# A gated cross-attention block on one core: the local stage's residual kept by tokens, the experts' outputs in halves, and free banks for the GLU

## The chip, the core and the metric

The kernel runs on one core of a Trainium2 chip. The core's engines are TensorE (PE, matrix products and transposes into the accumulator memory PSUM), VectorE (DVE), ScalarE (ACT), GpSimd (POOL) and SyncE (SP, which issues DMAs here). They run side by side, each through its own instructions in order, and wait for each other through semaphores. The metric is the device time of one execution in microseconds; lower is better.

## The reference

The input `x` is 16 batches (B) of 256 tokens (S) of 128 features (D). Everything is fp32. Four residual stages follow each other, each on the layer norm of `x` and scaled by tanh of a scalar gate:

```python
x = x + tanh(g_xattn[0]) * cross_attention_0(layernorm(x), ctx)   # 16 heads of 8, 64 keys
x = x + tanh(g_ffn[0])   * local_ffn(layernorm(x))
x = x + tanh(g_xattn[1]) * cross_attention_1(layernorm(x), ctx)   # with biases
x = x + tanh(g_ffn[1])   * experts(layernorm(x))

def local_ffn(x):                      # two layers of
    h = shift_token(x)                 # features 64..127 come from the token before
    q, k, v = split(h @ wqkv)          # 8 heads of 64
    q, k = rotary(l2norm(q) * qs, l2norm(k) * ks)
    x = x + window_attention(q, k, v) @ wo      # windows of 64 tokens
    h = layernorm(shift_token(x)) * lg + lb
    a, g = split(h @ w1 + b1)          # 341 hidden features each
    x = x + (a * gelu(g)) @ w2 + b2

def experts(x):                        # 4 experts of width 128, 4 of width 256
    w, sel = top_2(sigmoid(x @ router.T));  w = w / sum(w)
    return sum over the two chosen experts e of w_e * (relu(x @ w1_e)**2 @ w2_e)
```

All eight experts are computed for every token and weighted by `combine`, which is zero for those not chosen.

## The kernel before

The input stays in SBUF as `x_sb`, a tile of 128 tokens by 32 half batches by 128 features. One batch is two such half batches.

The order of the work is written into step tables (`CROSS_STEPS`, `LOCAL_STEPS`, `GLU_STEPS`, `EXPERT_STEPS` and others). A line names a step, the lag at which it runs behind its batch, its engine, a weight, the steps it needs, and the rooms (buffers or PSUM banks) that it takes, with the steps that give them back. `timetable` keeps one in-order queue of steps per stream (table) and engine, sorted by lag, and merges the streams greedily: whenever an engine is free it takes the first queue whose head has its needs and rooms, the earlier stream first. `play` issues the instructions in that order, so that each engine's order is fixed when the kernel is built. Three plays follow each other: the first cross attention, together with the preparation of weights and the first two norms of the local stage; the local stage; the second cross attention with the experts.

In the local play the streams are attention 0, GLU 0, attention 1, GLU 1, the other norms (`first`) and some clearing. A stream can be held until another has begun a step: `behind`. The GLUs are held until the attention of their layer has begun its last `scale1`; attention 1 is held until GLU 0 has begun the `shift` of the last batch.

The local stage's residual `yT` is kept transposed: features on partitions, 256 tokens of a batch along the free dimension. This is what each stage does with it, per batch:

- `first` norms `x_sb`, turns the result by two PE transposes (line 902) and copies it into `yT` on ACT (line 1176).
- Attention `shift` copies `yT` by two DMAs of SP (lines 1261 and 1262) into one of three `hbuf`, the second of them one token later. `qk` and `value` multiply it with `wqkv` (lines 1267 and 1297). At the end `project` (line 1445) multiplies the attention's result with `wo`, four matmuls of 256 columns, and `add` (line 1451) adds it to `yT`.
- GLU `shift` copies `yT` into one of two `gbuf` by two copies on POOL (lines 1245 and 1246). `hturn` transposes that back to tokens (line 902), `stat` (lines 1484, 1485) and `apply` (line 1495) make the norm from PSUM, `rstd` is on POOL (lines 1489, 1490), `nturn` transposes it again, `affine` is on ACT (line 1505), `up0` to `up2` (line 1521) are 12 matmuls of 256 columns, `gelu` and `gate` follow (lines 1531, 1539), `down` (line 1545) is three matmuls of 256 columns, and `out` (line 1551) adds it and the bias to `yT` on DVE.
- The last GLU also has `yturn`, which transposes `yT` to tokens, and `back` (line 1561), which adds it to `x_sb`.

Each fp32 matmul appears as two instructions in the trace. PSUM has banks named QK, SC, TR (two banks' width each), VB and OB. In the GLU's steady batches accumulator A (up0, up1) is always in QK, B (up2 and down) always in SC, and T, N and Y in other fixed ones.

In the experts `hid` makes 12 hidden blocks (line 1632), `out` (line 1654) multiplies them with the second weights, 24 instructions per half batch, into one tile of all eight experts. `sum` (line 1662) adds them to `x_sb` in eight DVE instructions, each an expert's output times its column of `comb`, and issues the output's DMA (line 1666).

Of the kernel before, what the change touches and what calls it, by code (L numbers as in the profile page):

```python
# [11 lines left out]
F32 = mybir.dt.float32  # L12
# [4 lines left out]
ALU = mybir.AluOpType  # L17
# [23 lines left out]
exp0 7 ACT 1.08 score_t pT:mix  # L41
mturn 2 PE 0.25 parts M:mturn_out
mturn_out 6 ACT 0.38 mturn mT:score_t
exp1 7 ACT 1.08 score_t,exp0
turn_out 4 ACT 0.38 turn xnT:query
rstd 2 POOL 1.03 stat
vals 5 POOL 0.32 - V:mix
refine 8 DVE 0.84 inverse
share 8 DVE 0.43 refine oT:project
log 7 ACT 0.38 mix  # L50
stat 2 DVE 0.92 - sm:apply
offset 3 DVE 0.16 rstd
top0 5 DVE 1.2 score
apply 2 POOL 1.02 offset xn:turn
score 1 PE 1.25 query_out,keys BIG:top0 BIG:top1
turn 0 PE 0.4 apply M:turn_out
keys 3 POOL 0.6 - Kd:score+score_t
mix 3 PE 1.8 exp0,exp1,vals O:share
inverse 7 ACT 0.38 log
top1 5 DVE 1.2 score,top0  # L60
parts 5 DVE 0.9 top0,top1 mp:mturn
add 8 DVE 0.48 project
query 0 PE 0.6 turn_out M:query_out
query_out 4 ACT 0.39 query QT:score+score_t
score_t 2 PE 1.2 mturn_out,query_out,keys BIG:exp0 BIG:exp1
project 4 PE 0.5 share M:add
"""

SECOND_STEPS = """
inverse 6 ACT 0.38 log  # L70
score 6 PE 1.25 query_out,keys BIG:top0 BIG:top1
apply 1 POOL 1.02 offset xn:turn
stat 3 DVE 0.92 - sm:apply
turn 5 PE 0.4 apply M:turn_out
top0 6 DVE 1.2 score
exp0 5 ACT 1.08 score_t pT:mix
mturn_out 4 ACT 0.38 mturn mT:score_t
exp1 5 ACT 1.08 score_t,exp0
mix 8 PE 1.8 exp0,exp1,vals O:share
rstd 0 POOL 1.03 stat  # L80
top1 6 DVE 1.2 score,top0
parts 6 DVE 0.9 top0,top1 mp:mturn
keys 0 POOL 0.6 - Kd:score+score_t
query 5 PE 0.6 turn_out M:query_out
offset 4 DVE 0.16 rstd
add 9 DVE 0.48 project
turn_out 2 ACT 0.38 turn xnT:query
score_t 7 PE 1.2 mturn_out,query_out,keys BIG:exp0 BIG:exp1
refine 8 DVE 0.84 inverse
share 8 DVE 0.43 refine oT:project  # L90
log 5 ACT 0.38 mix
vals 2 POOL 0.32 - V:mix
project 9 PE 0.5 share M:add
query_out 2 ACT 0.39 query QT:score+score_t
mturn 6 PE 0.25 parts M:mturn_out
# [3 lines left out]
hid2 4 PE 1.88 turn_out,hid1 BIG:relu2  # L99
stat 4 DVE 0.92 -  # L100
hid0 3 PE 1.88 turn_out BIG:relu0
prob 8 ACT 0.22 router
rstd 0 POOL 0.95 stat
apply 0 POOL 0.9 offset exn:turn
relu1 7 ACT 1.06 hid1,relu0
out0 5 PE 2.9 square0,square1,square2 BIG:sum0
turn_out 6 ACT 0.38 turn exnT:hid2+router
square0 7 ACT 1.04 relu0
sum1 8 DVE 1.95 out1,route
router 4 PE 0.45 turn_out O:prob  # L110
relu2 7 ACT 1.06 hid2,relu1
sum0 7 DVE 1.95 out0,route
out1 5 PE 2.9 square0,square1,square2 BIG:sum1
square2 7 ACT 1.04 relu2
square1 7 ACT 1.04 relu1
offset 4 DVE 0.16 rstd
route 6 DVE 2.7 prob cb:sum0+sum1
hid1 3 PE 1.88 turn_out,hid0 BIG:relu1
relu0 6 ACT 1.06 hid0 h:out0+out1
turn 2 PE 0.44 apply M:turn_out  # L120
# [4 lines left out]
xload0 6 LX 4.6 -  # L125
pturn 6 PE 0.35 pens BIG:pturn_out
cdup0 3 DVE 0.69 cturn0
pool 3 LP 5.0 -
cturn1 3 PE 0.9 cload1,cturn0 BIG:cturn_out1+cdup1
mload1 5 LM 7.0 mload0  # L130
vals2 9 PE 1.0 vals1,cdup1 BIG:vals_out2
vals1 6 PE 1.0 vals0 BIG:vals_out1
pturn_out 6 DVE 0.2 pturn
part 3 DVE 0.55 pload,dve
wload0 1 LW 5.4 -
fill1 9 DVE 0.65 mload1,fill0
keys_out1 8 ACT 0.61 keys1
wturn1 4 PE 0.4 wload1 BIG:wturn_out1
keys0 4 PE 1.8 wturn_out0,cturn_out0 BIG:keys_out0
fill0 7 DVE 0.28 part,mload0  # L140
heads 0 DVE 0.62 dve
wturn2 9 PE 0.25 wload2 BIG:wturn_out2
cturn_out1 1 ACT 0.61 cturn1
cturn_out0 0 ACT 0.61 cturn0
vals_out0 7 DVE 0.7 vals0
dve 1 LD 1.4 -
keys1 6 PE 0.95 cturn_out1 BIG:keys_out1
mload0 1 LM 7.0 -
wload1 1 LW 2.0 wload0
vals_out3 9 DVE 0.7 vals3  # L150
gates 7 ACT 0.3 act,pload
vals_out1 7 DVE 0.7 vals1
wturn_out0 0 ACT 0.38 wturn0
xload1 6 LX 2.0 xload0
wturn0 2 PE 0.8 wload0 BIG:wturn_out0
wturn_out1 2 ACT 0.25 wturn1
wturn_out2 9 ACT 0.25 wturn2
vals_out2 8 DVE 0.7 vals2
sels 5 DVE 0.3 heads
pload 2 LQ 6.2 -  # L160
cturn0 2 PE 1.0 cload0,wturn0 BIG:cturn_out0+cdup0
cload0 4 LC 5.4 -
keys_out0 3 ACT 0.61 keys0
unit 2 ACT 2.5 narrow,act
vals0 5 PE 1.3 wturn_out1,cdup0 BIG:vals_out0
narrow 0 DVE 0.38 dve
late 0 DVE 1.7 pool
nload 2 LN 10.0 -
cdup1 5 DVE 0.69 cturn1
cload1 4 LC 1.8 cload0  # L170
vals3 9 PE 1.0 vals2 BIG:vals_out3
wload2 1 LW 6.5 wload1
act 2 LA 3.0 -
pens 3 DVE 0.7 nload
# [3 lines left out]
keys1 2 PE 0.95 wturn_out BIG:keys_out1  # L178
vals_out3 3 DVE 0.7 vals3
rw 7 PE 0.15 - BIG:rw_out  # L180
vals2 9 PE 0.98 wturn_out BIG:vals_out2
vals_out1 5 DVE 0.7 vals1
cols 2 PE 0.15 - BIG:cols_out
keys_out1 2 DVE 0.75 keys1,cols_out
vals0 3 PE 0.98 wturn_out BIG:vals_out0
keys_out0 8 DVE 0.75 keys0,cols_out
vals_out0 3 DVE 0.7 vals0
rw_out 3 DVE 0.2 rw
bo_out 6 DVE 0.25 bo
bias 4 DVE 0.25 cols_out  # L190
vals1 7 PE 0.98 wturn_out BIG:vals_out1
bo 7 PE 0.4 bias,wturn_out BIG:bo_out
wturn 1 PE 0.6 - BIG:wturn_out
keys0 9 PE 0.95 wturn_out BIG:keys_out0
vals_out2 5 DVE 0.7 vals2
wturn_out 2 ACT 0.62 wturn
vals3 2 PE 0.98 wturn_out BIG:vals_out3
cols_out 0 DVE 0.35 cols
# [3 lines left out]
fill 3 DVE 1.2 -  # L202
local1 9 POOL 0.65 -
seen 0 DVE 1.0 -
tab2 9 DVE 0.5 -
tab3 3 DVE 0.5 -
tab1 3 DVE 0.5 -
local3 4 POOL 0.8 -
local0 1 POOL 0.98 -
tab0 8 DVE 0.5 -  # L210
local2 5 POOL 0.65 -
# [6 lines left out]
apply 1 POOL 0.9 offset hn:turn  # L218
turn 2 PE 0.3 apply VB:out
out 2 ACT 0.38 turn  # L220
# [9 lines left out]
add 5 DVE 0.42 project  # L230
norm0 2 POOL 0.87 root0
pturn_out1 5 ACT 1.02 pturn1 pT:mix1
mix_out0 5 ACT 0.62 mix0 oT:project
turn0 2 PE 0.995 scale0 TR:turn_out0
score1 3 PE 1.24 turn_out1,turn_out0 SC:exp1+top1
total0 3 DVE 1.4 exp0
pturn1 4 PE 1 share1 TR:pturn_out1
mix0 4 PE 1.07 pturn_out0,dma0 OB:mix_out0
share1 4 POOL 1.9 total1
scale0 2 POOL 1.05 rotate0,norm0  # L240
qk1 1 PE 1.75 shift QK:square1+sin1+cos1
rotate1 2 POOL 2.56 sin1,cos1
clip1 2 POOL 0.27 sums1
exp1 4 ACT 2.6 top1 pr:pturn1
dma0 8 DMA0 2.5 value_out0
value0 2 PE 0.911 shift VB:value_out0
pturn0 3 PE 1 share0 TR:pturn_out0
root0 2 ACT 0.45 clip0
sin0 1 DVE 1.21 qk0 u:rotate0
norm1 2 POOL 0.87 root1  # L250
shift 3 DMA2 2.6 - hb:qk0+qk1+value0+value1
cos0 1 DVE 1.21 qk0 qn:turn0
pturn_out0 4 ACT 1.02 pturn0 pT:mix0
mix1 4 PE 1.07 pturn_out1,dma1,dma0 OB:mix_out1
mix_out1 5 ACT 0.62 mix1,mix_out0
square1 2 ACT 1.04 qk1 sq:sums1
share0 3 POOL 1.9 total0
scale1 2 POOL 1.05 rotate1,norm1
top1 3 DVE 1.4 score1,norm1
clip0 1 POOL 0.27 sums0  # L260
turn_out1 3 ACT 1.02 turn1
score0 2 PE 1.24 turn_out0 SC:exp0+top0
rotate0 1 POOL 2.56 sin0,cos0
sums0 1 DVE 1.22 square0
turn1 2 PE 0.995 scale1 TR:turn_out1
sin1 1 DVE 1.21 qk1 u:rotate1
exp0 3 ACT 2.6 top0 pr:pturn0
value_out0 2 DVE 0.7 value0 v:mix0+mix1
project 4 PE 1.69 mix_out0,mix_out1 OB:add
total1 3 DVE 1.4 exp1  # L270
top0 2 DVE 1.4 score0,norm0
square0 1 ACT 1.04 qk0 sq:sums0
turn_out0 2 ACT 1.02 turn0 qT:score0+score1
root1 2 ACT 0.45 clip1
value1 2 PE 0.911 shift VB:value_out1
cos1 1 DVE 1.21 qk1 qn:turn1
qk0 0 PE 1.75 shift QK:square0+sin0+cos0
sums1 1 DVE 1.22 square1
value_out1 2 DVE 0.7 value1
dma1 9 DMA1 2.5 value_out1  # L280
"""
GLU_STEPS = """
up0 2 PE 0.96 affine A:gate0+gate1
gate0 4 DVE 0.48 gelu0
up1 2 PE 0.96 affine,up0
down 3 PE 1.45 gate0,gate1,gate2
gate1 4 DVE 0.48 gelu1,gate0
out 5 DVE 0.48 down
shift 6 POOL 1.25 - hg:hturn
rstd 7 POOL 0.95 stat  # L290
stat 2 DVE 0.92 hturn
gelu1 3 ACT 0.47 up1,gelu0
affine 2 ACT 0.5 nturn hnT:up0+up1+up2
gelu2 3 ACT 0.47 up2,gelu0
gelu0 2 ACT 0.47 up0 hh:down
nturn 1 PE 0.44 apply N:affine
gate2 4 DVE 0.48 gelu2,gate0
hturn 0 PE 0.44 shift T:apply
apply 2 DVE 0.82 rstd hn:nturn
up2 2 PE 0.95 affine B:out  # L300
"""
LAST_GLU_STEPS = """
gate1 2 DVE 0.48 gelu1,gate0
stat 0 DVE 0.92 hturn
rstd 3 POOL 0.95 stat
up1 2 PE 0.96 affine,up0
nturn 1 PE 0.44 apply N:affine
hturn 0 PE 0.44 shift T:apply
gelu2 5 ACT 0.47 up2,gelu0
gelu0 4 ACT 0.47 up0 hh:down  # L310
gate2 2 DVE 0.48 gelu2,gate0
up2 2 PE 0.95 affine B:out
apply 0 DVE 0.82 rstd hn:nturn
back 3 DVE 0.48 yturn
yturn 3 PE 0.44 out Y:back
shift 2 POOL 1.25 - hg:hturn
out 2 DVE 0.48 down
up0 1 PE 0.96 affine A:gate0+gate1
gate0 1 DVE 0.48 gelu0
# [1459 lines left out]
```

## Time and profile before

| what | value |
|---|---|
| times of three runs | 1162.91, 1167.99, 1166.86 us (median 1166.86) |
| profiled execution, its own time | 1164.6 us |
| its span in the profile | 1162.8 us |
| granted TensorE clock, mean | 0.989 |
| busy: PE / weight loads / DVE / ACT / POOL | 1080.4 / 786.3 / 940.2 / 734.9 / 630.9 us |
| DMA | 30.02 MB, mean 26 GB/s |

Stages by the trace: first cross attention until about 140 us, attention 0 until 430, GLU 0 until 517, attention 1 from 490 to 776, GLU 1 until 858, second cross attention until 989, experts from 957 to the end.

The profile was taken from one execution. Engine names are those above, PEld is TensorE's weight load, SPq the queue in which SP issues DMAs. "L1521" is line 1521 of the kernel before. In a timeline line the columns are start, duration, engine, line, operation, output from inputs, shapes, number of instructions, and in brackets the idle time of the engine before it with what ended it. In a line of windows each engine's busy time stands with its number of instructions, then the granted clock (1.00 is full), the DMA engines' busy share, and GB/s.

### The profile page before, as it was taken

What the parts mean: (1) busy time and instruction counts of PE and PEld (TensorE: products, weight loads), DVE (VectorE), ACT (ScalarE), POOL (GpSimd) and SP (SyncE); (2) the same over time, 40 slices, a digit from 0 to 9 for tenths busy, and PEclk for the clock granted to TensorE, in tenths of its full rate; (3) what the DMA queues carried; (4) which work ended last, traced back from release to release, by engine and by line L of the source; (5) the groups of instructions that cost most, each with busy time, mean ns of one, the idle gap of its engine ahead of it and who ended that gap; (6) DMA issues with size and microseconds to landing.
All of it is one profiled execution on the core that took longest, in us unless ns stands there. A gap on an engine that the chain in (4) does not pass through costs nothing.

```text
span 1162.8 us, 28289 instructions
## 1 busy us (share of the span) xinstructions
PE 1080.4 (93%) x11264; PEld 786.3 (68%) x11264; DVE 940.2 (81%) x2088; ACT 734.9 (63%) x1418; POOL 630.9 (54%) x1079
## 2 busy tenths in 40 slices
PE   7999878999999999888999999999979999999997
PEld 5555535766767777655667767677645557999996
DVE  7887679999999856679999999856757884777777
ACT  4555447888888863357888888853335557555462
POOL 5443179999988833258888888733345460111110
PEclk9999989999999999999999999999989999999999
DMA  6400011111111100001111111100000000000000
GB/s 182 143 2 2 10 24 33 33 29 38 37 31 36 29 10 10 1 14 33 37 30 37 38 34 33 29 7 1 1 1 2 2 1 2 12 13 12 13 12 17
DMA packets 29828, 30.02 MB, mean 26 GB/s; under 512 B 4668, under 2 KB 22656, under 8 KB 29696
## 3 DMA queue, kind: packets, MB, share of 16 engines
q1 hardware_dynamic: 28352, 27.56, 9.4%
q8 instruction: 89, 1.46, 0.5%
q10 hardware_dynamic: 1344, 0.66, 0.2%
q14 instruction: 43, 0.35, 0.1%
HBM read 9.33 MB, written 2.10 MB: 10 GB/s over the span
## 4 chain that ended last, share of the span: by engine, by line
PE 70%; DVE 18%; ACT 6%; issue 4%; POOL 1%; DMA 1%; SPq 0%; DVEq 0%; ACTq 0%; POOLq 0%
PE QK L1267 8%; PE e_y L1654 8%; PE e_h_ps L1632 7%; PE po L1115 5%; PE Ag L1521 4%; PE OB L1427 4%; PE TR L1415 3%; PE SC L1374 3%; ACT pr L1397 3%; DVE mx L1383 3%; PE VB L1297 3%; PE OB L1445 3%; PE TR L1346 3%; DVE qn L1278 3%; PE sT L1092 2%
## 5 line engine op out<-in xcount | busy, mean ns | idle before, releaser
L1397 ACT ACTIVATE pr<-SC,mx,rn 128x128 f32<-128x128 f32 x512 | 185.6, 468 | 36.1 <-DVE mx L1388 36.0
L1267 PE MATMUL QK<-wqkv,hbuf 128*128 128x512 f32 x256 | 129.5, 629 | 19.3 <-DVE qn L1278 14.2
L1410 POOL TENSOR_TENSOR pr<-pr,rs 128x1024 f32<-128x1024 f32 x64 | 121.4, 1896 | 14.7 <-DVE rs L1405 11.4
L1662 DVE SCALAR_TENSOR_TENSOR x_sb<-e_y,e_comb,x_sb 128x128 f32<-128x128 f32 x256 | 89.1, 349 | 21.6 <-PE e_y L1654 13.7
L1644 ACT ACTIVATE e_h<-e_h_ps 128x1024 f32<-128x1024 f32 x48 | 49.2, 1025 | 77.2 <-PE e_y L1654 61.8
L1267 PEld LDWEIGHTS QK<-wqkv,hbuf 128*128 128x128 f32 x256 | 44.6, 193 | 77.8 <-issue 40.2
L1654 PE MATMUL e_y<-mw,e_h 128*128 128x128 f32 x768 | 91.8, 277 | 0.0
L1632 PE MATMUL e_h_ps<-e_xnT,mw 128*128 128x256 f32 x384 | 89.8, 383 | 0.2
L1654 PEld LDWEIGHTS e_y<-mw,e_h 128*128 128x128 f32 x768 | 89.2, 192 | 0.7
L1040 DVE TENSOR_REDUCE nm<-sc 128x16 f32<-128x1024 f32 x64 | 75.0, 1214 | 14.2 <-PE sc L1031 14.0
L1275 ACT ACTIVATE sq<-QK 128x1024 f32<-128x1024 f32 x64 | 65.9, 1030 | 31.8 <-ACT pr L1397 9.0
L1312 POOL TENSOR_TENSOR qn<-qn,u 128x512 f32<-128x512 f32 x64 | 81.3, 1271 | 8.6 <-DVE qn L1278 6.0
L1278 DVE TENSOR_TENSOR u<-QK,tab 128x1024 f32<-128x1024 f32 x64 | 76.9, 1201 | 9.3 <-ACT sq L1275 5.4
L1102 ACT ACTIVATE xpT<-sT,penT 128x1024 f32<-128x1024 f32 x64 | 71.3, 1117 | 20.3 <-PE sT L1092 20.3
L1404 DVE TENSOR_REDUCE rs<-pr 128x8 f32<-128x1024 f32 x64 | 77.6, 1212 | 7.9 <-ACT pr L1397 5.3
L1383 DVE TENSOR_REDUCE mx<-SC 128x8 f32<-128x1024 f32 x64 | 77.5, 1212 | 6.3 <-PE SC L1374 6.3
L1313 POOL TENSOR_TENSOR qn<-qn,u 128x512 f32<-128x512 f32 x64 | 81.6, 1275 | 0.0
L1418 ACT COPY pT<-TR 128x1024 f32<-128x1024 f32 x64 | 64.4, 1007 | 24.0 <-PE TR L1415 24.0
L1278 DVE TENSOR_TENSOR qn<-QK,tab 128x1024 f32<-128x1024 f32 x64 | 77.6, 1213 | 1.1 <-ACT sq L1275 1.1
L1292 DVE TENSOR_REDUCE ss<-sq 128x16 f32<-128x1024 f32 x64 | 77.1, 1205 | 1.1 <-ACT sq L1275 1.1
L1632 PEld LDWEIGHTS e_h_ps<-e_xnT,mw 128*128 128x128 f32 x384 | 70.4, 190 | 10.9 <-DVE x_sb L1662 2.7
L1531 ACT ACTIVATE hhg<-Ag,cols 128x256 f32<-128x256 f32 x64 | 28.7, 472 | 72.7 <-PE Ag L1521 36.4
(217 smaller groups left out, 2644.8 us busy)
## 6 DMA issues: line engine op xcount, KB each, us to landing
vbuf<-vbuf SPq DMA_DIRECT2D x96, 128.0 KB
hbuf<-yT SPq DMA_DIRECT2D x32, 64.0 KB
out_dram<-x_sb SPq DMA_DIRECT2D x32, 64.0 KB
hbuf<-yT SPq DMA_DIRECT2D x32, 63.8 KB
wqkv<-in_L_ffn_wqkv_dram SPq DMA_DIRECT2D x2, 768.0 KB
mw<-in_L_ffn_w_dram SPq DMA_DIRECT2D x2, 768.0 KB
w<-in_L_ffn_w_dram SPq DMA_DIRECT2D x2, 341.0 KB
x_sb<-in_x_dram SPq DMA_DIRECT2D x1, 640.0 KB
```

The lines of the kernel that those rows point to most:

```text
L1267: nc.tensor.matmul(ps[:, 512 * j : 512 * j + 512], lhsT=hbuf[b % 3][:, W + t * P : W + (t + 1) * P], rhs=wqkv[:, l, 512 * j : 512 * j + 51 ...
L1278: nc.vector.tensor_tensor(work(tag, b, t, [P, 2, LH, LD], 2, wp), live["QK", b, t].rearrange("p (q h d) -> p q h d", q=2, h=LH), tab[:, l, ...
L1292: nc.vector.tensor_reduce(ss, live["sq", b, t].rearrange("p (g d) -> p g d", d=LD), AX.X, ALU.add)
L1312: nc.gpsimd.tensor_add(qg[:, :, 0:32], qg[:, :, 0:32], ug[:, :, 32:64])
L1313: nc.gpsimd.tensor_add(qg[:, :, 32:64], qg[:, :, 32:64], ug[:, :, 0:32])
L1383: nc.vector.tensor_reduce(mx, live["SC", b, t].rearrange("p (g c) -> p g c", c=P), AX.X, ALU.max, negate=True,)
L1397: nc.scalar.activation(pr[:, g, :], live["SC", b, t][:, g * P : (g + 1) * P], AF.Exp, bias=live["mx", b, t][:, g : g + 1], scale=live["rn" ...
L1404: nc.vector.tensor_reduce(rs, live["pr", b, t], AX.X, ALU.add)
L1410: nc.gpsimd.tensor_tensor(pr, pr, rs, ALU.mult)
L1632: nc.tensor.matmul(ps[:, c * S : (c + 1) * S], lhsT=mw1[:, (4 * j + c) * P : (4 * j + c + 1) * P], rhs=live["xnT", b], start=True, stop=True,)
L1654: nc.tensor.matmul(y[:, e * D : (e + 1) * D], lhsT=live["h", b][:, c, t * P : (t + 1) * P], rhs=mw2[:, c, :], start=(c == cs[0]), stop=(c ...
L1662: nc.vector.scalar_tensor_tensor(xt, live[f"y{t}", b][:, e * D : (e + 1) * D], live["comb", b][:, t, e : e + 1], xt, ALU.mult, ALU.add,)
```

## The change

It has five parts.

1. **The residual by tokens.** `yT` becomes `y_sb`, tokens on partitions as in `x_sb`. The first norms write `y_sb` directly, without transposes and ACT copy. In the attention the two DMAs are replaced by `hturn`, two PE transposes into bank VB, and `hout`, two ACT copies of 64 partitions into `hbuf`. `project` becomes eight matmuls of 128 columns with the weights as the moving side. In the GLU the copies on POOL and `hturn` are replaced by three DMAs of SP into `gbuf`, which now has tokens on partitions; `stat` and `apply` read `gbuf` in SBUF. `down` becomes six matmuls of 128 columns, the bias b2 is added to `y_sb` by a new step `bias` on POOL from a copy of b2 on all partitions (one more DMA at the start), `out` is a plain add, and `yturn` is gone: `back` reads `y_sb`.
2. **The GLU's accumulators** A and B take any of QK, SC and TR that is free (fewer at the two ends), N any of VB and OB.
3. **The release.** Attention 1 is held only until GLU 0 has begun its fifth `shift`.
4. **The experts' outputs in halves.** `out` becomes four steps, the narrow and the wide experts of each half batch. For each, `weigh` multiplies a half (128x512) with `comb`, broadcast, in one DVE instruction from PSUM into SBUF, and `gather` adds its four parts and `x_sb` in three POOL instructions; the output's DMA follows the second half. Four buffers for `weigh` (room `w`).
5. **All step tables are re-ordered**: new lags and rows, so the merge differs in places in every stage.

```diff
-    behind = (2 * l - 1, "shift", B - 1) if l else None
+    behind = (2 * l - 1, "shift", 4) if l else None
...
-    dict(A="QK", B="SC", T="VB", N="OB", Y="OB"),
+    (("QK", "SC"), ("TR", "VB")), (("QK", "SC", "TR"), ("VB", "OB")), (("TR", "SC"), ("OB", "VB")),
...
         # attention
-        def shift(b, t):
-            h = hbuf[b % 3]
-            nc.sync.dma_start(h[0:64, W : W + S], yT[0:64, b, :])
-            nc.sync.dma_start(h[64:128, W + 1 : W + S], yT[64:128, b, 0 : S - 1])
+        def hturn(b, t):
+            turn(acc("VB", b, t, 512), y_sb[:, b])
+        def hout(b, t):
+            h, ps = hbuf[b % 3], live["VB", b, t]
+            nc.scalar.copy(h[0:64, :], ps[0:64, 0:S])
+            nc.scalar.copy(h[64:128, 1:S], ps[64:128, 0 : S - 1])
...
         # GLU
         def shift(b, _):
-            shifted(yT, b, gbuf[b % 2])
-        def hturn(b, _):
-            turn(acc("T", b), gbuf[b % 2].rearrange("p (t q) -> p t q", t=2))
+            g, y = gbuf[b % 2], y_sb[:, b]
+            nc.sync.dma_start(g[:, :, 0:64], y[:, :, 0:64])
+            nc.sync.dma_start(g[1:P, :, 64:D], y[0 : P - 1, :, 64:D])
+            nc.sync.dma_start(g[0:1, 1, 64:D], y[P - 1 : P, 0, 64:D])
...
+        def bias(b, _):
+            y = y_sb[:, b]
+            nc.gpsimd.tensor_tensor(y, y, b2[:, l].unsqueeze(1).to_broadcast([P, 2, D]), ALU.add)
...
         def out_(b, _):
-            nc.vector.scalar_tensor_tensor(
-                yT[:, b, :], live["B", b][:, 512 : 512 + S], cols[:, 16 + l : 17 + l],
-                yT[:, b, :], ALU.add, ALU.add,
-            )
+            nc.vector.tensor_add(y, live["B", b][:, 512 : 512 + S], y)
...
         # experts
-        def sum_(b, t):
-            xt = x_sb[:, 2 * b + t, :]
-            for e in range(E):
-                nc.vector.scalar_tensor_tensor(
-                    xt, live[f"y{t}", b][:, e * D : (e + 1) * D], live["comb", b][:, t, e : e + 1],
-                    xt, ALU.mult, ALU.add,
-                )
-            nc.sync.dma_start(out_v[:, 2 * b + t, :], xt)
+        def weigh(b, j):
+            t, half = j // 2, j % 2
+            nc.vector.tensor_tensor(
+                work(f"w{j}", b, [P, 4, D], 4, wp, tag="e_w"),
+                live[f"y{t}", b][:, 512 * half : 512 * half + 512]
+                .rearrange("p (e d) -> p e d", e=4),
+                live["comb", b][:, t, 4 * half : 4 * half + 4].unsqueeze(2)
+                .to_broadcast([P, 4, D]), ALU.mult,
+            )
+        def gather(b, j):
+            w, xt = live[f"w{j}", b], x_sb[:, 2 * b + j // 2, :]
+            nc.gpsimd.tensor_add(w[:, 0:2, :], w[:, 0:2, :], w[:, 2:4, :])
+            nc.gpsimd.tensor_add(w[:, 0, :], w[:, 0, :], w[:, 1, :])
+            nc.gpsimd.tensor_add(xt, xt, w[:, 0, :])
+            if j % 2:
+                nc.sync.dma_start(out_v[:, 2 * b + j // 2, :], xt)
...
         # a step table, as an example: the GLU's lines for the steps around gbuf
-shift 6 POOL 1.25 - hg:hturn
-hturn 0 PE 0.44 shift T:apply
-stat 2 DVE 0.92 hturn
-apply 2 DVE 0.82 rstd hn:nturn
+shift 0 DMA2 2.8 - hg:apply
+stat 0 DVE 0.92 shift
+apply 1 DVE 0.6 rstd hn:nturn
```

In the changed kernel the room of a `gbuf` (`hg`, two of them) is given back by `apply`, since `stat` and `apply` read it directly; before it was given back by `hturn`.

## The prediction

> **What bounds the kernel now.** I read the page's busy times first, then the chain that ended last, then busy time by windows, one per stage.
>
> ```profile
> PE 1080.4 (93%) x11264; PEld 786.3 (68%) x11264; DVE 940.2 (81%) x2088; ACT 734.9 (63%) x1418; POOL 630.9 (54%) x1079
> ```
> ```profile
> PE 70%; DVE 18%; ACT 6%; issue 4%; POOL 1%; DMA 1%; SPq 0%; DVEq 0%; ACTq 0%; POOLq 0%
> ```
> ```profile
> 435.00:475.00 40.00, 36.04 (x174) 29.40 (x175) 24.67 (x80) 14.85 (x32) 13.35 (x32) 1.00 0.03 7
> ...
> 555.00:634.00 79.00, 79.00 (x945) 55.78 (x944) 76.30 (x87) 66.63 (x141) 65.17 (x91) 1.00 0.16 36
> 870.00:940.00 70.00, 63.80 (x886) 36.89 (x878) 55.22 (x147) 42.26 (x74) 36.47 (x75) 0.99 0.01 2
> 1000.00:1140.00 140.00, 139.75 (x952) 129.22 (x951) 103.00 (x432) 75.76 (x97) 20.80 (x46) 1.00 0.04 13
> 1143.00:1163.00 20.00, 11.20 (x101) 11.01 (x99) 15.71 (x56) 3.31 (x5) 0.00 (x0) 0.87 0.06 17
> ```
> The windows' columns are PE, PEld, DVE, ACT, POOL. Second attention (555 to 634) and experts (1000 to 1140) are full of matmul: work taken off PE there shortens them, work added lengthens them, and DVE with 76.30 of 79 is close behind. First GLU (435 to 475) and second cross attention leave PE a tenth idle, so something else holds them. After 1154 PE is done and DVE ends the kernel.
>
> In the GLU the timeline shows the holder:
>
> ```profile
> 450.12 0.48 DVE L1551 SCALAR_TENSOR_TENSOR yT<-Bg,cols,yT 128x256 f32<-128x256 f32 x1
> ...
> 450.65 1.10 PE L1521 MATMUL Bg<-hnTg,w 128*85 128x256 f32 x4 [0.50 <-DVE yT L1551]
> 451.59 1.89 PE L1521 MATMUL Ag<-hnTg,w 128*128 128x256 f32 x8
> ...
> 453.31 1.46 PE L1545 MATMUL Bg<-hhg,w 128*128 128x256 f32 x6
> ```
> Bank B is one fixed bank: the next batch's up2 waits until `out` has read it, and PE idles 0.50 us. Starts of up2 are 5.05 us apart; in the second GLU the starts of `down` in the chain are 5.29 apart (790.36, 795.65). Second attention's projections start 15.72 apart.
>
> **GLU after.** PE per batch is up 2.61 (1.73+0.87), down 1.34 (12 instructions of 0.112, the cadence of 128-column matmuls in the expert stage) and nturn 0.27: 4.21 us; `hturn` and `yturn` are gone. Banks are no longer fixed and stop mattering. Next comes a loop through the new DMAs. There are two `gbuf`, so shift of batch k+2 starts when `apply` of k has read its buffer, and `stat` of k+2 stands in DVE's in-order queue ahead of `apply` of k+1. The built order on DVE is apply 8, three gates, stat 10, out 5, apply 9. So the period is X + stat + out + apply, with X from apply's end to the landing of all three DMAs. stat is 0.91 (two pairs of 0.272 and 0.181), out 0.45, apply 0.65 (0.72 now from PSUM), hops 0.1. In the second GLU the order is apply 9, out 6, back 6, three gates, stat 11, apply 10: out, back and gates (0.45+0.47+1.44) lie under X.
>
> X is the only number no row has. The nearest rows are the attention's shift of the same tensor:
>
> ```profile
> 568.96 0.46 SPq L1261 DMA_DIRECT2D hbuf<-yT  x1
> 569.48 0.59 SPq L1262 DMA_DIRECT2D hbuf<-yT  x1
> ```
> ```profile
> DMA  0000000000000004798300026983100000008896
> ...
> q1 hardware_dynamic: 192, 0.20, 25.9%
> ```
> The second row is the DMA view from 568.9 to 572 in 40 slices: the first transfer moves until about 570.5, the second until 571.1, so each has ended 1.6 us after its issue began; their landings are recorded at 1.9 to 2.0. Second shift DMA: issue begins 0.56 after apply, lands 2.0 to 2.2 later, 2.55 to 2.75. Third, of one row: begins 1.2, and the smallest transfer in the trace (an output tile) lands 1.53 after issue: 2.7. I take X = 2.85, with a hop at each side. Bounds: 2.65 if the DMAs behave just as hbuf's; 3.65 if 256 short runs cost as much each as the 64 of 1 KB (0.259 × 16 engines × 3.1 us / 192 packets = 0.067 each; 16 per engine instead of 4 is 0.8 more). I take the lower half because total bytes are equal and the output's 512 B packets last 0.027, not 0.067.
>
> The Trainium skill, "DMA: Bandwidth & Descriptors", in the section on the anatomy of one DMA, gives about 2.0 us fixed plus bytes; its specifications ask for at least 512 B per transfer, which speaks against 256-byte rows. The 1.9 us landing agrees with the first; nothing here shows the second. With 2.0 from the third issue, an estimate from that page, X would be 3.3 and 12 us of the sum below would go.
>
> First GLU: 2.85+0.91+0.45+0.65+0.1 = 4.96 against 5.05, 12 steady batches: **−1**. Second GLU: 2.85+0.91+0.65+0.1 = 4.5 against 5.29, 15 periods: **−12**. Bias on POOL (nearest row 755 ns, 128x256) joins 0.93 us of rstd in a 4.5 us period and the two POOL copies (0.39, 0.40) go: no cost.
>
> **Attentions.** `hturn` adds two transposes (0.12 each, 0.25), project goes from 8 instructions in 1.73 to 16 of 0.112 in 1.79: +0.32 per batch. hout (two copies, the yT copy's row is 372 ns) lies where ACT idled 0.82 after its root; bank VB is free there; SP's two DMAs of 1.05 issue leave. PE is full in the second attention: 16 × 0.32 = **+5**. In the first, two transposes of the first norms leave (14 of them within it): +0.07 per batch, **+1**. DVE is nearly full there too, but gains no instruction.
>
> **Release by the fifth shift.** It looks like a large overlap, since PE idles 10.7 of the 55 us between 490 and 545. The built order gives little of it: the second attention's first qk moves only from after GLU 0's down 12 to before down 11, since the GLU is the earlier stream in the list and both want bank QK: **−1**; bounds 0 and −6.
>
> **Start and first cross attention.** Re-ordered lags put offset 0 ahead and the first score 1 to 2 us earlier (now 15.27); a b2 broadcast joins SP's queue: **−2**, bounds −3 and +1. Both cross attentions keep their PE order, hence their period.
>
> **Into and out of the experts.** `hid0` of batch 0 now stands before mturn 12, inside the second cross attention, where PE waits for the residual add (0.57 each in the waits): **−1**, bounds −3 and +2 as either table's waits lengthen. Steady, 24 instructions of e_y and 12 of e_h per tile keep the same time: PE-bound at 11.49 per batch, and unchanged. DVE loses 16 sums of 349 ns and gains 4 weighings of 685 (the row of another 128x512 from PSUM): 5.58 to 2.74 per batch, hidden. POOL gains 6 us per batch on top of 20.8 in 140: hidden.
>
> The "GPSIMD Engine Reference" calls GpSimd the wrong engine for ordinary elementwise work. POOL's 621 ns for 128x256 agrees that it is slow; it would matter only if more than some 9 us per batch came to it.
>
> **The tail.** Now 8.6 us from the last matmul to the end: 16 sums, 0.35 plus gaps, 6 us, then issue and DMA 2.5. After: the last half's weighing 0.69, POOL's three adds for it (some 0.6+0.45+0.45, plus part of the half before), DMA 2.5: 5.2. **−3.4.**
>
> Sum: −1 −12 +5 +1 −1 −2 −1 −3.4 = −14.4. The profiled execution took 1164.6 (span 1162.8), so 1150.2 on its scale; of the runs shown the median lies 2.3 above that execution and the lowest 1.7 below, so I take **1151**.
>
> **Rivals.** (a) Slower: X is long, through short descriptors. Each us of X costs 12+15 = 27 us, so the gain is gone at X = 2.85+14.4/27 = 3.38; at X = 4.2 the kernel takes 1151+36 = 1187. For: three chained issues and 256-byte runs, none in the trace. Against: equal bytes, DMA engines 3% busy. (b) Nothing to measure: X 3.2 to 3.6, or X as forecast with another 10 us lost where the attention's DVE and ACT, both re-ordered, fall behind PE (DVE has 2.70 of 79 us spare): 1161 to 1172. (c) More: the release fills PE's idle time and the experts' early start the cross attention's: 6 and 3 more, 1141.
>
> **Chances.** Forecast 0.52 (its own range 1146 to 1158), (c) 0.14, (b) 0.13, (a) 0.21. The range takes in (c), and of (a) the part up to X = 3.75: 1139 to 1175. Half a per cent, 5.8 us, is about what a measurement of this kernel can tell: faster 0.66, same 0.13, slower 0.21.
>
> **What would show it.** Starts of up2 4.96 apart in the first GLU and `down` 4.5 apart in the second, with stat waiting for gbuf's DMA; projections 16.04 apart in the second attention; experts 11.49; end 5.2 after the last matmul. stat waiting with GLU periods over 5.3 means (a); projections over 16.3 apart means (b); second qk's run within GLU 0 means (c).

## The result and the profile after

The changed kernel takes 1243.14 us (median of four runs, 1241.72 to 1245.29) against 1165.04 us for the kernel before: 1.067 times as long, 95% interval 1.0637 to 1.0703. That is 78 us more; 14 less were forecast. Its profiled execution took 1243.03 us with a span of 1241.3, 78.5 longer than the span before.

Read in the order of the prediction, the page's busy times and chain come first.

```profile
PE 1099.7 (89%) x11648; PEld 816.6 (66%) x11648; DVE 890.8 (72%) x1896; ACT 752.8 (61%) x1466; POOL 738.7 (60%) x1239
...
PE 51%; DMA 13%; DVE 12%; issue 4%; POOL 3%; ACT 3%; SPq 2%; POOLq 0%; DVEq 0%; ACTq 0%
```

PE's work grew by 19 us, but its share of the chain fell from 70% to 51%, and 13% is now DMA, which had 1%. The list of waits over the whole run names it (engine and line, what ended the wait, us in total, times, longest):

```profile
DVE stg L1491 <- DMA gbuf<-y_sb: 122.1, 33, 5.4
```

In the windows (PE, PEld, DVE, ACT, POOL, then clock, DMA share, GB/s), these are the steady first GLU, the second attention, the experts and the last 20 us:

```profile
455.00:495.00 40.00, 29.37 (x133) 22.35 (x131) 14.15 (x50) 10.06 (x23) 8.26 (x15) 0.87 0.08 17
600.00:679.00 79.00, 77.33 (x944) 55.57 (x943) 72.89 (x83) 67.57 (x145) 62.51 (x89) 1.00 0.11 25
1075.00:1215.00 140.00, 139.59 (x986) 131.56 (x979) 73.76 (x293) 78.91 (x101) 99.11 (x192) 1.00 0.04 12
1222.00:1242.00 20.00, 10.65 (x92) 10.36 (x90) 6.61 (x21) 3.86 (x4) 12.83 (x24) 0.86 0.05 14
```

In the first GLU every engine is idle much of the time, and even the granted clock falls to 0.87. One batch of it in the timeline of the changed kernel:

```profile
456.96 0.59 DVE L1502 TENSOR_SCALAR hng<-gbuf,mvg,rstdg 128x128 f32<-128x128 f32 x2
...
457.62 0.65 SPq L1483 DMA_DIRECT2D gbuf<-y_sb  x1
...
458.31 0.70 SPq L1484 DMA_DIRECT2D gbuf<-y_sb  x1
...
459.05 2.73 SPq L1485 DMA_DIRECT2D gbuf<-y_sb  x1
...
463.79 0.29 DVE L1491 BATCH_NORM_STATS2 stg<-gbuf 128x6 f32<-128x128 f32 x1 [5.06 <-DMA gbuf<-y_sb]
```

`apply` ends at 457.55, the three DMAs follow, and `stat` starts at 463.79: X, the time from apply's end until the next contents of its buffer can be read, is 6.2 us, where 2.85 was forecast with a bound of 3.65. The DMA view of the same stretch, 457.5 to 464 in 40 slices (busy share of the 16 DMA engines in tenths, GB/s, and packets), shows why:

```profile
DMA  0000000019600000000000000000001100000000
GB/s 0 0 0 0 0 0 0 0 27 243 134 0 0 8 9 17 17 19 17 19 17 19 17 19 17 19 17 19 17 19 19 19 17 19 17 19 3 0 0 0
DMA packets 559, 0.13 MB, mean 20 GB/s; under 512 B 559, under 2 KB 559, under 8 KB 559
```

The first transfer moves 64 KB at up to 243 GB/s in three slices. The second, nearly as large, creeps at 17 to 19 GB/s for 3.6 us. The packets can be counted out: 256 runs of the first, 254 of the second, 16 pieces of the third make 526, and 33 are left. Read as one completion for each engine that takes part in a DMA, these are 16 for the first, 16 for the third, and **one** for the second: its 127 partitions went through a single DMA engine. The busy share agrees: up to nine tenths of the 16 engines in the first transfer, and under one tenth while the second creeps. The experiments below test this reading.

From the starts of matmuls in the timelines, the 78.4 us of the unrounded spans divide so (forecast in brackets): first cross attention −2.7 (start −2); first attention, to its thirteenth projection, +5.0 (+1); from there to the last `down` of the first GLU +37.2 (−1); to the second attention's first projection +1.8 and through twelve of its periods +7.0 (−1 and +5); to the end of the second GLU +32.7 (−12); to the second cross attention's first projection +1.4; from there to the last expert batch −4.0 (−1); tail 0.0 (−3.4).

### The profile page after: what moved, and what is told of

It is laid out like the page before. It is cut to its first block, busy times and chain, and to the rows that moved or that the text cites. A ratio compares the mean times of both kernels' runs of the same rounds, so it can differ in the third digit from the quotient of the medians.

```text
span 1241.3 us, 29279 instructions
## 1 busy us (share of the span) xinstructions
PE 1099.7 (89%) x11648; PEld 816.6 (66%) x11648; DVE 890.8 (72%) x1896; ACT 752.8 (61%) x1466; POOL 738.7 (60%) x1239
## 4 chain that ended last, share of the span: by engine, by line
PE 51%; DMA 13%; DVE 12%; issue 4%; POOL 3%; ACT 3%; SPq 2%; POOLq 0%; DVEq 0%; ACTq 0%
DMA gbuf<-y_sb 13%; PE QK L1271 9%; PE e_h_ps L1636 7%; PE e_y L1661 7%; PE OB L1431 4%; PE TR L1419 4%; PE SC L1378 4%; DVE qn L1282 3%; PE VB L1301 2%; DVE mx L1387 2%; PE TR L1350 2%; PE po L1123 2%; POOL rstdg L1497 2%; PE SC L1365 1%; PE sc L1039 1%
## 5 line engine op out<-in xcount | busy, mean ns | idle before, releaser
L1414 POOL TENSOR_TENSOR pr<-pr,rs 128x1024 f32<-128x1024 f32 x64 | 121.5, 1899 | 10.3 <-DVE rs L1409 10.3
L1496 POOL TENSOR_SCALAR rstdg<-mvg 128x2 f32<-128x2 f32 x32 | 7.1, 222 | 174.1 <-DVE mvg L1492 174.1
L1491 DVE BATCH_NORM_STATS2 stg<-gbuf 128x6 f32<-128x128 f32 x64 | 17.8, 278 | 122.1 <-DMA gbuf<-y_sb 122.1
L1669 DVE TENSOR_TENSOR e_w<-e_y,e_comb 128x512 f32<-128x512 f32 x64 | 43.4, 685 | 76.2 <-PE e_xnT_ps L910 35.0
L1279 ACT ACTIVATE sq<-QK 128x1024 f32<-128x1024 f32 x64 | 65.8, 1029 | 26.9 <-PE QK L1271 12.8
L1557 PE MATMUL Bg<-w,hhg 128*128 128x128 f32 (+1 forms) x384 | 58.8, 311 | 24.2 <-DVE hhg L1546 23.6
```

Of the source, the lines that this page charges most:

```text
L1414: nc.gpsimd.tensor_tensor(pr, pr, rs, ALU.mult)
```

## The experiments

Two theories stood against each other. T1: a transfer of 127 partitions is carried by one engine. T2: runs of 256 bytes are slow in themselves. Behind both stood a question of order: is the wait only as costly as it is because `stat` stands ahead of `apply` in DVE's queue? Ratios are to the kernel before, with 95% intervals.

**The second transfer cut in two.**

```diff
-            nc.sync.dma_start(g[1:P, :, 64:D], y[0 : P - 1, :, 64:D])
+            nc.sync.dma_start(g[1:113, :, 64:D], y[0:112, :, 64:D])
+            nc.sync.dma_start(g[113:P, :, 64:D], y[112 : P - 1, :, 64:D])
```

> The changed kernel with GLU's second shift DMA, 127 partitions, cut in two: 112 partitions and 15. Nothing else is changed. Theory T1 (a transfer of 127 partitions is carried by a single DMA engine, since 127 cannot be dealt evenly over 16: the trace shows 17 to 19 GB/s for 3.5 us and 1 completion packet instead of 16): the long transfer goes, X (apply's end to stat's start) falls from 6.2 to 3.6 to 4.0 us, GLU periods from 7.95 and 7.64 to 5.3 to 5.7 and 5.1 to 5.5, time about 1243 - 27 x 2.4 = 1178 (1168 to 1192). Rival T2 (256-byte runs are slow in themselves, or the number of runs is): the bytes and runs are the same, a fourth DMA is issued, and the time stays within 10 us of 1243 or grows.

Measured: 1174.97 us, ratio 1.0077 (1.0052 to 1.0102). One more DMA and the same bytes in the same runs take 68 us away. X falls to 3.6 in about half of the batches and to 3.8 to 6.3 in the others, and the GLUs' periods are 5 to 6.7 and 5.1 us. The DMA view from 455.5 to 461 has three bursts and a short fourth:

```profile
GB/s 0 0 0 0 0 0 0 0 0 0 52 264 155 6 0 71 244 97 6 0 0 0 49 8 0 0 1 2 0 0 0 0 0 0 0 0 0 0 0 0
DMA packets 589, 0.13 MB, mean 24 GB/s; under 512 B 589, under 2 KB 589, under 8 KB 589
```

589 less 526 leaves 63 completions: 16, 16 for the 112, 15 for the 15, 16. T1 holds, T2 falls. Of the 3.6 us, the four issues take 2.8, one behind the other (0.67, 0.62, 0.91 and 0.59).

**No shift at all.**

```diff
-            nc.sync.dma_start(g[1:P, :, 64:D], y[0 : P - 1, :, 64:D])
-            nc.sync.dma_start(g[0:1, 1, 64:D], y[P - 1 : P, 0, 64:D])
+            nc.sync.dma_start(g[:, :, 64:D], y[:, :, 64:D])
```

> The changed kernel with the second shift DMA over all 128 partitions, unshifted, and without the third: the second half of the features is taken from the token itself, not from the token before. 256 runs of 256 bytes each, one DMA less. T1: X is issue 0.65, issue 0.70 and a landing of 1.3 to 1.8 after it: 2.8 to 3.2; GLU periods 4.9 to 5.2 and 4.4 to 4.8; time 1243 - 27 x 3.2 = 1157 (1147 to 1168), which is the prediction's own X. T2: X stays above 5 and the time above 1210.

This kernel leaves the token shift out, so its result is another one and only its time counts. Measured: 1154.81 us, ratio 0.9896 (0.9864 to 0.9927). Timeline of this kernel, one batch:

```profile
458.50 0.34 DVE L1501 TENSOR_SCALAR hng<-gbuf,mvg,rstdg 128x128 f32<-128x128 f32 x1
458.91 0.59 SPq L1483 DMA_DIRECT2D gbuf<-y_sb  x1
459.55 0.61 SPq L1484 DMA_DIRECT2D gbuf<-y_sb  x1
...
461.56 0.29 DVE L1490 BATCH_NORM_STATS2 stg<-gbuf 128x6 f32<-128x128 f32 x1 [0.25 <-DMA gbuf<-y_sb]
```

X is 2.7, close to the 2.65 that the prediction gave to DMAs "just as hbuf's", with 512 runs of 256 bytes, though with one DMA fewer. PE's own floor shows: `down` is 4.41 us apart in most of the first GLU, where PE is busy for all of the 40 us from 435 to 475, and 4.37 and 4.82 by turns in the second. With both transfers on 16 engines, and the one-row DMA left out, the forecast of 1151 is 4 us off. That closeness is in part luck: by the same starts of matmuls the first GLU gained 10.7 us where 1 was forecast, while the attentions lost 12.8 instead of 6 and the tail gained nothing.

**The order of stat and apply.**

```diff
 # GLU_STEPS
+apply 1 DVE 0.6 rstd hn:nturn
 stat 0 DVE 0.92 shift
...
-apply 1 DVE 0.6 rstd hn:nturn
 # LAST_GLU_STEPS
+apply 4 DVE 0.6 rstd hn:nturn
 stat 3 DVE 0.92 shift
...
-apply 4 DVE 0.6 rstd hn:nturn
```

> The changed kernel with one line of each GLU table moved: apply ahead of stat of the same step, so that on DVE apply of batch k+1 no longer stands behind stat of batch k+2, which waits for the shift. The DMAs stay as they are, one engine for 127 partitions. If the cost is the loop (a wait in DVE's in-order queue ahead of the apply that frees the next buffer), the same X of 6.2 us is spread over two batches: (6.2 + stat 0.9 + rstd 1.3 + apply 0.6)/2 = 4.5 to 5.0 per batch, time 1243 - 12 x 3.1 - 15 x 2.8 = 1164 (1155 to 1178). If instead the DMA's own throughput or SP's issue (4.2 us of issue per batch) bounds it, periods stay above 5.5 and the time above 1185.

Measured: 1178.22 us, ratio 1.0104 (1.0071 to 1.0138), at the upper end of the loop's forecast. X is still 6.2 in most batches, and 65 us are gone: periods fell from 7.95 to 4.4 to 5.2 and from 7.64 to 5.1 to 5.2. X counts half when two batches' loops run beside each other. So the slow transfer cost its 78 us only together with an order that made every `apply` wait for the transfer of the batch after it.

**Both cures.** The cut at 112 and the moved line together.

> Both cures: the second transfer cut into 112 and 15 partitions, and apply ahead of stat. X 3.8 over two batches is under PE's 4.4 per batch, so the GLUs are bound by PE as in the run without a shift: periods 4.4 and 4.4 to 4.8, time 1148 to 1157, below the kernel before. If the four DMA issues (2.8 us) or their reading of y_sb get in the way of bias and out, 1160 or more.

Measured: 1160.38 us, ratio 0.9937 (0.9916 to 0.9957): below the kernel before, 3 above the range. `down` is 4.41 apart in the first GLU and mostly 4.37 and 4.82 by turns in the second, as without a shift; in the first, PE is busy all the time (40.00 of the 40 us from 445). So the cut transfer is worth 68 us in the old order and 18 in the new one. What the range missed does not lie in the GLUs' steady periods: from the first attention's thirteenth projection to the second attention's first it takes 155.3 us, and 149.8 without a shift; why was not settled.

**How many engines a count of partitions gets.**

```diff
-            nc.sync.dma_start(g[1:P, :, 64:D], y[0 : P - 1, :, 64:D])
+            n = (120, 96, 126, 64)[b % 4]
+            nc.sync.dma_start(g[1 : n + 1, :, 64:D], y[0:n, :, 64:D])
+            nc.sync.dma_start(g[n + 1 : P, :, 64:D], y[n : P - 1, :, 64:D])
```

> The changed kernel with the second shift cut at 120, 96, 126 or 64 of the 127 partitions, by batch number modulo 4, to read from the trace how many engines carry each piece (completion packets, rate). If a DMA is dealt out by the largest power of two or divisor up to 16 of its partitions: 96 and 64 on 16 engines, 120 on 8 or 15, 126 on 2 or 14, and 63, 31, 7 and 1 on 1, or as their divisors give (9, 7). If 127 was slow for another reason, such as the offset of one partition between source and destination, the pieces of 96 and 64 are slow too.

Measured: 1180.13 us (one run). Packets in the DMA views of four successive batches, cut at 64, 120, 96 and 126:

```profile
DMA packets 583, 0.13 MB, mean 28 GB/s; under 512 B 583, under 2 KB 583, under 8 KB 583
```
```profile
DMA packets 582, 0.16 MB, mean 28 GB/s; under 512 B 580, under 2 KB 580, under 8 KB 580
```
```profile
DMA packets 575, 0.13 MB, mean 27 GB/s; under 512 B 575, under 2 KB 575, under 8 KB 575
```
```profile
DMA packets 576, 0.15 MB, mean 31 GB/s; under 512 B 574, under 2 KB 574, under 8 KB 574
```

Of the packets under 512 B (two larger ones in the second and the fourth belong to another transfer), 526 are data and 32 the completions of the first and third DMA. Left are 25, 22, 17 and 16: 16+9 for 64 and 63 partitions, 15+7 for 120 and 7, 16+1 for 96 and 31, 14+2 for 126 and 1 (the single partition has two runs). Each fits the largest divisor up to 16 (for the single partition, of its two runs); 31 and 127 are prime and get one. An offset of one partition does no harm.

**The release undone.** `(2 * l - 1, "shift", 4)` back to `B - 1`.

> The changed kernel with the second attention released by the last shift as before. The prediction priced the release at -1 (0 to -6), so the time is 1243 to 1249, 1 expected more. Rival: since GLU 0 is now a wait for DMAs, its idle PE is where an early second attention could run, and the release is worth more than forecast: 1250 to 1263. Third: the early attention only puts its vbuf DMAs and its DVE work into GLU 0's way, and the time falls by 3 to 10.

Measured: 1249.52 us, ratio 1.0716 (1.0688 to 1.0743). The release is worth 6.4 us here (5.4 by the ratios), at the far end of its bounds and just short of the rival's range, in a kernel whose first GLU leaves PE idle; what it is worth where PE is full was not run.

**The experts' part alone**, in the kernel before.

> The kernel before with the experts' part alone: out in halves, weigh on DVE, gather on POOL, the new table of the experts and four buffers. The prediction priced it at -3.4 (tail) and -1 (overlap): 1160 to 1163. The trace of the changed kernel has experts 11.20 apart instead of 11.49, which over 14 batches would be 4 more: 1156 to 1159. Rival: POOL's adds, now 77 us of the expert stage, slow DVE or the second cross attention, and nothing or a loss is left: 1165 or more.

Measured: 1165.07 against 1165.78 us, ratio 0.9972 (0.995 to 0.9995). From the second cross attention's first projection to the last matmul its trace takes 267.8 us, the kernel before 270.8; the stretch behind the last matmul is 8.6 us in both. Experts are 11.20 apart instead of 11.49, and the hand-over gives part of it back (the first period is 14.76 instead of 11.66). The median lies where the rival has it and above both forecasts; by the ratio the gain is 0.6 to 5.8 us, and none of it is in the tail.

**hturn behind score1**, on top of both cures: the line `hturn` with lag 1 behind `score1`, one place later on PE.

> split_reorder with hturn one place later in PE's order, behind score1 instead of ahead of it; nothing else moves in the attentions. Theory A: hturn costs more than its 0.25 us because it stands in the chain turn_out, score1, mx, exp, where DVE waits 0.79 us for the scores; then the second attention's projections fall from 16.33 apart to 16.0 to 16.1, and the time by 4 to 8. Theory B: the 16.33 come from DVE's mx times rn (1.50 us while POOL's share runs) and its order against POOL: no change within 2. Theory C: hout comes later and qk waits for it: 3 to 8 slower.

Measured: 1159.15 us, ratio 0.994 (0.991 to 0.9969), projections still 16.33 apart. Theory A falls: this place of `hturn` costs nothing.

**POOL's order in the attentions put back**, on top of both cures.

```diff
+share1 5 POOL 1.9 total1
 scale0 3 POOL 1.05 rotate0,norm0
...
-share1 5 POOL 1.9 total1
...
-clip1 3 POOL 0.27 sums1
 rotate1 3 POOL 2.56 sin1,cos1
+clip1 3 POOL 0.27 sums1
...
-share0 4 POOL 1.9 total0
 norm1 3 POOL 0.87 root1
+share0 4 POOL 1.9 total0
```

> split_reorder with the attentions' order on POOL put back to that of the kernel before: share1 ahead of scale0, rotate1 ahead of clip1, norm1 ahead of share0. PE, ACT and DVE keep their orders. Theory B: DVE's mx times rn cannot end while POOL's share runs (it takes 1.50 us then, 0.22 otherwise), and share begins 1.0 us later because scale0 (1.04 us) stands ahead of it; put back, the projections go from 16.33 to 16.05 apart, 3 to 5 us per attention, 6 to 9 us in all: 1151 to 1154. Theory D: the 0.3 us come from PE's longer chain alone (score0 reaches DVE 0.5 later): no change within 2.

Measured: 1150.7 us, ratio 0.9869 (0.9838 to 0.99), 9.7 us below both cures (7.9 by the two ratios, since the runs of the kernel before beside them differ by 1 us). The projections of the second attention are 15.74 apart, as in the kernel before. First the timeline with both cures, then that with POOL's order put back:

```profile
613.17 1.04 POOL L1344 TENSOR_TENSOR qn<-qn,rn 128x512 f32<-128x512 f32 x1
614.17 1.90 POOL L1414 TENSOR_TENSOR pr<-pr,rs 128x1024 f32<-128x1024 f32 x1
614.59 1.50 DVE L1392 TENSOR_TENSOR mx<-mx,rn 128x8 f32<-128x8 f32 x1
616.01 1.21 DVE L1282 TENSOR_TENSOR qn<-QK,tab 128x1024 f32<-128x1024 f32 x1
```
```profile
610.94 1.90 POOL L1414 TENSOR_TENSOR pr<-pr,rs 128x1024 f32<-128x1024 f32 x1
611.96 0.90 DVE L1392 TENSOR_TENSOR mx<-mx,rn 128x8 f32<-128x8 f32 x1
612.78 1.21 DVE L1282 TENSOR_TENSOR qn<-QK,tab 128x1024 f32<-128x1024 f32 x1
612.80 1.05 POOL L1344 TENSOR_TENSOR qn<-qn,rn 128x512 f32<-128x512 f32 x1
```

In these rows L1414 is the step `share`, L1344 is `scale0`, and DVE's L1392 multiplies the scores' maxima. This product of 128 by 8 elements ends within 0.02 us of POOL's share in both (616.09 and 616.07; 612.86 and 612.84). Where POOL takes `scale0` first, share starts 1 us later, DVE is held for 1.50 us, and the next `qn` and `qk` come late. Three rows were moved together, so the run shows that POOL's order is the cause and these rows show a way; `share1` alone was not moved. The Trainium skill, "SBUF — State Buffer", section "SBUF: two separate sides", has the rule: a DVE instruction with two SBUF inputs and a GpSimd instruction that reads SBUF exclude each other for a whole instruction. The rows agree.

**The cures together**: the cut at 126 and 1, the moved lines, and for the last batch `gather` on DVE.

```diff
+            on = nc.vector if b == B - 1 else nc.gpsimd
-            nc.gpsimd.tensor_add(xt, xt, w[:, 0, :])
+            on.tensor_add(xt, xt, w[:, 0, :])
```

The other two adds are changed in the same way. First with POOL's order as in the changed kernel:

> split_reorder with the second transfer cut at 126 and 1 instead of 112 and 15, and the three adds of gather on DVE for the last batch alone. The tail: after the last matmul weigh 0.69, three adds on DVE some 0.9, issue and DMA 2.5: 4.2 instead of 8.7, so 4 to 5 less; the cut gives 0 to 1, since the GLUs are bound by PE already: 1154 to 1157. If the tail is held elsewhere (POOL still busy with batch 14), 2 less.

Measured: 1156.56 us, ratio 0.9908 (0.9877 to 0.9939), inside the range, though the tail gave less than forecast (below). Then with POOL's order put back:

> best2 with the order on POOL of sr_pool: the sum of both, 1146 to 1150 under theory B, 1154 to 1157 under D.

Measured: 1147.94 us, ratio 0.9836 (0.9805 to 0.9867): 1.6% below the kernel before and 7.7% below the changed one. Behind the last matmul both kernels still take 7.5 us: some 1.2 were gained instead of 4 to 5. DVE's own weigh and adds, 1.7 us for each half, are now in line, and the first of them still wait for the buffers of `weigh` (`e_w`) that POOL's backlog holds.

## Why the prediction was wrong

**The step that failed is X.** The sum had the loop right: with the measured X it gives periods of 8.3 and 7.9 us, and 7.95 and 7.64 were measured. The prediction put the price at 27 us for each us of X; with 6.2 that is −14.4 + 27 × 3.35 = +76, and +78 was measured. That the two agree so closely is in part luck: the two GLUs took 69.9 us more where this gives 77, and the other stages 8.5 more where the sum has 1.4 less. What showed it right was also named: `stat` waiting for gbuf's DMA with periods over 5.3 us meant rival (a). But X was put together from the landing of two DMAs of 64 partitions, and its upper bound priced the packets, never the number of engines that share them. The bound of 3.65 took for granted 16 engines ("16 per engine"); with one, 254 packets at some 14 ns make 3.6 us by themselves. The third DMA's issue took 2.73 us behind it, instead of the 0.6 that the last issue takes in most batches of the cut kernels. A smaller part of the step stays open: no run has the three DMAs with each on many engines, and with four X is 3.6 or more, at the prediction's upper bound, so 2.85 is not shown for the shift as written.

**The worry about 256-byte runs was misplaced.** The row without a shift (X 2.7) shows no loss by them, against the page's 512 B line as the prediction weighed it: they moved at up to 261 GB/s, hbuf's runs of 1 KB at up to 237. The page of the Trainium skill that it drew on, "DMA: Bandwidth & Descriptors", states the missed rule in another section, "Why a DMA increments its semaphore by 16 and not by 1": a DMA takes the largest number up to 16 that divides the slowest dimension, of more than one element, of both its patterns, and 127 partitions get one. All counts measured here agree. The 127 stands in the diff; the prediction counted "256 short runs" in each transfer, as of 128 partitions. The 2.0 us that it took from the page's section on the anatomy of one DMA are given there for DMAs issued from GpSimd; these are issued by SP, and nothing of the sum rests on them.

**The first GLU's floor** is 4.41, not 4.21 and not 4.96: with the shift left out, or with both cures, PE binds it. One cure alone leaves it at 4.4 to 6.7.

**The attentions** (+6 forecast, about +12 measured): the right sign for the wrong reason, and half the size. Two transposes and a longer projection cost nothing that can be seen in the second attention once POOL's order is put back (15.74 against 15.73): before, PE lost some 0.28 us per batch in small waits, most of it at `qk`, by the starts of its matmuls, and these are gone. What cost 0.6 us per batch there is a part of the change that the sum has no term for: the new order on POOL, by the rows above `share` behind `scale`. Rival (b) named the re-ordered DVE and ACT; it was POOL, through DVE. Of the first attention's +5.0, 3.5 lie ahead of its first projection and stay when POOL's order is put back; their cause is open.

**The tail** (−3.4 forecast, 0.0 measured) failed at "part of the half before": POOL has 1.75 us for each of four halves in line behind one another, 7 us, and DVE waits for their buffers. **The experts** were held unchanged at 11.49 and run at 11.20. The trace before shows why: once per batch the weight load of `hid` waits 0.21 us for DVE's last `sum` to give its bank back (13 times between 1000 and 1140, 2.7 us), and one step within `out` takes 0.08 longer. In the changed kernel neither is there. The prediction called this stage bound by PE and left that wait out. **The start** (−2.7) and **the release's sign** were right, the release at its bound.

## What to carry to other kernels

Look at the number of partitions of every new DMA: a prime count above 16, or another without a large divisor up to 16, moves through few engines, and one partition less than 128 can make a transfer eight times as long. A wait for a DMA should stand behind, not ahead of, the work that frees the next buffer in the same in-order queue: moving one line in each of two tables was worth 65 of 78 us here. Count a change of order on POOL as a cost wherever DVE reads two SBUF operands beside it.

## What the runs showed of the hardware that was not expected

A DMA from SBUF to SBUF of 127 partitions ran at 17 to 19 GB/s on one engine; the 128-partition one of the same run length reached 243. The completion packets (1 instead of 16) told the number of engines in these traces.

Behind the 254 runs that drained through one engine the next DMA's issue on SP took 2.7 to 2.8 us instead of 0.6, so that the queue of issues was held too. Behind the 31 partitions on one engine (62 runs) it took 0.6 in seven of eight batches.

A DVE instruction of 128x8 elements with two inputs in SBUF took between 0.17 and 1.7 us. In the changed kernel 35 of the 64 took over 0.4 us, and each of these ended within 0.03 us of the end of a product on POOL: 28 times the one of 128x1024, seven times one of 128x512.
